# The order of emission in a convolution, attention and mixing kernel: a 3x3 input transform issued step by step, and a prologue whose parts are interleaved

## The chip, the cores and the metric

The kernel runs on one core of one Trainium2 chip. The time is device microseconds of one execution; of several executions the median is given. A core has a matrix engine (TensorE, PE), a vector engine (VectorE, DVE), a scalar engine (ScalarE, ACT), a general engine (GpSimd, POOL) and a sync engine (SyncE, SP) that here only issues DMA transfers. PE writes into PSUM, of which this kernel uses eight banks of 128 x 512 float32; everything else lies in SBUF or in the chip's main memory.

## The reference

Two layers work on eight images of 512 channels and 32 x 32 pixels, all in float32.

```python
# layer 0
x = x + C2f(group_norm(x))
# C2f: t = silu(bn(conv1x1(x))); y0, y1 = two halves of t, 256 channels each
for i in range(2):
    z = silu(bn(conv3x3(y[-1], m_cv1_w[i])))
    q, k, v = conv1x1(z, m_qkv_w[i])             # 4 heads of 64 channels, 1024 positions
    a = softmax(q . (k + rw + rh) * 64 ** -0.5)
    z = silu(bn(conv1x1(a . v, m_cv2_w[i])))
    y.append(y[-1] + z)
out = silu(bn(conv1x1(concat(y), cv2_w)))
# layer 1
x = x + L1(group_norm(x))
# L1: a 1x1 convolution whose weights are scaled by the largest softmax value of each row of S and T,
#     masked where the argmax of S and of T differ, and whose outputs are permuted by p[p], p = argsort(t)
```

Group norm has 32 groups of 16 channels.

## The kernel before, in words

Every image passes the two attention blocks i = 0 and 1. A pair (image, block) is a slot. Images go in pairs, so the order of slots is (0,0), (1,0), (0,1), (1,1), (2,0) and so on, 16 in all. The main loop (from L918) does the attention of slot s in four units: two head pairs times two halves of the query positions. A unit takes eight key tiles. For each, `logits` (L446) makes two logits matmuls into PSUM banks, ACT copies them to SBUF (L459), and DVE takes the running maximum `mx` (L464), which is the last reader of the bank. `top` and `spread` turn the maxima by PE (L472, L480). `soften` (L482) adds the negative maximum on DVE (L484), exponentiates on ACT (L485) and sums on POOL (L490). `values` multiplies by v (L496), and `finish` and `divide` apply the reciprocal of the sum (L508 to L517). DVE's maxima and additions are tied to each other in their order by hand (`in_turn`, L430).

Between the steps of the attention of slot s the loop takes work from `slot_filler` (L824): everything that slot s + 1 needs before its own attention. In order: 8 us of background work; if the next block is 1, the output projection `conv_m2(0)` (L351) and 9 us more of background work; the 3x3 convolution `conv3` (L223); `conv_m2(1)` or 7 us of background work; the projection to q, k and v (`project`, L312); and background work for the rest of a share of 103 us. Background work (`bg.take`) is the first convolution of later images (`First`), the last convolution of layer 0 (`Second`) and layer 1 (`Last`). All of these are Python generators that yield an estimate of the PE time that they have just issued, and a clock of those estimates (`Clock`, L661) starts entries at a given delay (`clock.at`). So the text of the program decides in which order operations are emitted. A framework then plans each engine's own order and all waits; it doesn't keep to the order of emission.

The 3x3 convolution works on groups of four rows in a transformed space (a minimal filtering scheme along the rows). Six input planes u0 to u5 are formed from `ybuf`, the zero-padded image in SBUF, by eight DVE operations for u1 to u4 (L266 to L277) and two on POOL and two on DVE for u0 and u5 (L284 to L287). Each plane goes through 12 matmuls with its transformed weights (`product`, L239) into one bank. Sums and differences of the products (`ss`, `dd`, L288 to L300) give the four output rows y[0] to y[3], and a silu ends it. There are four plane buffers and three buffers for the temporaries a, b, a2, b2. For block 0 `ybuf` is loaded from memory (`load_y`, L217); for block 1 `conv_m2(0)` writes it (L365).

The prologue (L860 to L915) treats images 0 and 1 in turn: load, group norm statistics, normalization, first convolution (`start_conv`). Image 0's conv3 follows, then `positions` (position terms to memory), `last_weights` (L567: layer 1's weights; one-hot masks, ranks and permutations, with four groups of PE work at L605, L609, L624 and L639 to L646), the transformed 3x3 weights of block 1 (`transform_weights`, L544), the first convolution of a half of image 2, and the first `project` and logits. Pools that matter here: ten `st` tiles for logits, which the weights also use; four weight tiles `w`; three half tiles for silu results; five PSUM banks for everything but v's product and the spread maxima.

Of the kernel before, what the change touches and what calls it, by code (L numbers as in the profile page):

```python
# [39 lines left out]
def conv_preact_kernel(ctx: ExitStack, tc: tile.TileContext, x, cv1, cv2, mcv1, qkv, mcv2, bn, rw, rh, conv, s_in, t_in, out):  # L40
# [130 lines left out]
    def accumulate(ps, terms):  # L171
# [6 lines left out]
        return Whole(1.72)  # L178

    class Image:  # L180
        def __init__(self, n):
# [39 lines left out]


        def conv3(self, i):  # L223
            n = self.n
            name = f"{n}_{i}"
            groups = ybuf.rearrange("p c r x -> p (c r x)").rearrange("p (g r x) -> p g r x", r=4, x=F)
            d = [groups[:, 0:NGR, r] for r in range(4)] + [groups[:, 1 : NGR + 1, r] for r in range(2)]

            def temp(nm):
                return wt.tile([P, NGR, F], F32, tag="wt", name=f"{nm}_{name}")  # L230

# [31 lines left out]
            mm, ss, dd = (pair(wm, q, f"{q}_{name}") for q in ("mm", "ss", "dd"))  # L263

            a, b = temp("a"), temp("b")
            stt(a, d[2], -4.0, d[4], ALU.mult, ALU.add)  # L266
            stt(b, d[1], -4.0, d[3], ALU.mult, ALU.add)
            u1, u2 = plane(), plane()
            nc.vector.tensor_tensor(inner(u1), a, b, ALU.add)
            nc.vector.tensor_tensor(inner(u2), a, b, ALU.subtract)  # L270

            a, b = temp("a2"), temp("b2")
            nc.vector.tensor_tensor(a, d[4], d[2], ALU.subtract)
            nc.vector.tensor_tensor(b, d[3], d[1], ALU.subtract)
            u3, u4 = plane(), plane()
            stt(inner(u3), b, 2.0, a, ALU.mult, ALU.add)
            stt(inner(u4), b, -2.0, a, ALU.mult, ALU.add)  # L277
            yield from product(1, u1)
            nc.scalar.copy(mm[:, 0], self.ps)
            yield 1.33  # L280
            yield from product(2, u2)

            u0, u5 = plane(), plane()
            nc.gpsimd.tensor_tensor(inner(u0), d[0], d[2], ALU.subtract)  # L284
            nc.gpsimd.tensor_tensor(inner(u5), d[5], d[3], ALU.subtract)
            stt(inner(u0), inner(u0), 4.0, a, ALU.mult, ALU.add)
            stt(inner(u5), b, -4.0, inner(u5), ALU.mult, ALU.add)  # L287
            nc.vector.tensor_tensor(ss[:, 0], mm[:, 0], self.ps, ALU.add)  # L288
            nc.vector.tensor_tensor(dd[:, 0], mm[:, 0], self.ps, ALU.subtract)
            yield 1.33  # L290
            yield from product(3, u3)
            nc.scalar.copy(mm[:, 1], self.ps)
            yield 1.33
            yield from product(4, u4)
            nc.vector.tensor_tensor(ss[:, 1], mm[:, 1], self.ps, ALU.add)
            nc.vector.tensor_tensor(dd[:, 1], mm[:, 1], self.ps, ALU.subtract)
            stt(y[1], tx(dd[:, 1]), 2.0, tx(dd[:, 0]), ALU.mult, ALU.add)
            stt(y[2], tx(ss[:, 1]), 4.0, tx(ss[:, 0]), ALU.mult, ALU.add)
            nc.vector.tensor_tensor(ss[:, 0], ss[:, 0], ss[:, 1], ALU.add)
            stt(dd[:, 0], dd[:, 1], 8.0, dd[:, 0], ALU.mult, ALU.add)  # L300
            yield 1.33
            yield from product(0, u0)
            nc.vector.tensor_tensor(y[0], tx(self.ps), tx(ss[:, 0]), ALU.add)
            yield 1.33
            yield from product(5, u5)
            nc.vector.tensor_tensor(y[3], tx(self.ps), tx(dd[:, 0]), ALU.add)
            for co in range(IT):
# [259 lines left out]
    def last_weights():  # L567
# [31 lines left out]
        nc.vector.tensor_tensor(lower, gi, wide(idx), ALU.is_gt)  # L599

        oht = pair(stp, "st", "oht")[:NG]
        for a in range(2):
            ps = bank(f"oht_{a}")
            for k in range(CT):
                nc.tensor.transpose(ps[:NG, ts(k, P)], oh[:, CT * a + k], ident)  # L605
            nc.vector.tensor_copy(oht[:, a], ps[:NG])
        for k in range(CT):
            ps = bank(f"mask_{k}")
            nc.tensor.matmul(ps, oht[:, 1, ts(k, P)], oht[:, 0], start=True, stop=True)  # L609
            wk = weff[k // 2][:, k % 2]  # L610
            stt(wk, wk, gain[:, CT + k : CT + k + 1], ps, ALU.mult, ALU.mult)


        tri = small.tile([P, P], F32, tag="tri", bufs=1, name="tri")
# [18 lines left out]
        for k in range(CT):  # L633
            nc.vector.tensor_scalar(perm[k // 2][:, k % 2], io[:, 0], rank[:, k : k + 1], None, ALU.is_equal)
        w1 = [pair(stp, "st", f"w1_{j}") for j in range(2)]
        for o in range(CT):
            ps = bank(f"w1_{o}")
            for k in range(CT):
                nc.tensor.matmul(  # L639
                    ps, perm[k // 2][:, k % 2, ts(o, P)], weff[k // 2][:, k % 2], start=(k == 0), stop=(k == CT - 1)  # L640
                )
            nc.vector.tensor_copy(w1[o // 2][:, o % 2], ps)
        for i in range(CT):
            ps = bank(f"w2_{i}")
# [167 lines left out]
    def call(f, *a):  # L812
        f(*a)
        return
        yield
# [8 lines left out]
    def slot_filler(s):  # L824
# [49 lines left out]
    def start_norm(im, tiles):  # L874
        im.gn0.mean()
        im.gn0.var()
        for h in range(2):
            im.norm_x([tiles[h, kp] for kp in range(2)])

    def start_conv(im, tiles):  # L880
        n = im.n
        for cp in (1, 0):
            w = weights(f"w_cv1_{n}_{cp}", (CT, 256), cv1[cp])
            for h in range(2):
                for co in range(IT):
                    ps = bank(f"cv1_{n}_{cp}_{co}_{h}")
                    us = yield from accumulate(ps, [(w[:, k, ts(co, P)], tiles[h, k // 2][:, k % 2]) for k in range(CT)])
                    t = half_tile(f"y0_{n}_{cp}_{co}_{h}")
# [144 lines left out]
```

## Time and profile before

| quantity | value |
|---|---|
| median of 3 runs (lowest to highest) | 3366.42 us (3352.67 to 3372.92) |
| profiled execution: own time, span | 3359.56 us, 3357.8 us |
| PE, share of the span busy | 95% |
| DVE, ACT, POOL | 62%, 53%, 37% |
| granted PE clock, mean | 0.98 of full |
| first logits matmul | 219.39 us after the start |
| input transform, one operation of 128 x 544 | 0.72 us, up to 1.80 us |

Times in the profile are microseconds from the start of the span unless a column says nanoseconds. A line of the timeline has start, duration, engine, source line, operation, what it writes and reads, and in brackets how long the engine was idle ahead of it and which instruction ended that. A line of waits has the waiting engine and line, the releaser, the total, the number and the longest. PE's float32 matmuls count as two records each. A line of the table by stretch has the stretch, its length, the busy time of each engine with its instructions, the granted PE clock, the share of the DMA engines and GB/s.

### The profile page before, as it was taken

What the parts mean: (1) busy time and instruction counts of PE and PEld (TensorE: products, weight loads), DVE (VectorE), ACT (ScalarE), POOL (GpSimd) and SP (SyncE); (2) the same over time, 40 slices, a digit from 0 to 9 for tenths busy, and PEclk for the clock granted to TensorE, in tenths of its full rate; (3) what the DMA queues carried; (4) which work ended last, traced back from release to release, by engine and by line L of the source; (5) the groups of instructions that cost most, each with busy time, mean ns of one, the idle gap of its engine ahead of it and who ended that gap; (6) DMA issues with size and microseconds to landing.
All of it is one profiled execution on the core that took longest, in us unless ns stands there. A gap on an engine that the chain in (4) does not pass through costs nothing.

```text
span 3357.8 us, 33292 instructions
## 1 busy us (share of the span) xinstructions
PE 3185.7 (95%) x11716; PEld 1549.4 (46%) x11716; DVE 2074.0 (62%) x2717; ACT 1764.3 (53%) x2371; POOL 1237.1 (37%) x971
## 2 busy tenths in 40 slices
PE   6999989999999999999999999999999999999998
PEld 2645435353545445354545445354545445353343
DVE  4335666576766576676766675776656675766642
ACT  3035685755564654644555555644455554645631
POOL 2004333344443344334444343344334333444420
PEclk9899999999999999999999999999999999999999
DMA  7553343230222341432222341423232341423366
GB/s 273 211 176 128 109 152 110 96 118 34 101 92 93 104 138 46 146 109 101 101 101 94 122 144 54 138 100 110 91 109 93 116 144 54 155 72 107 110 212 204
DMA packets 142294, 400.34 MB, mean 119 GB/s; under 512 B 13104, under 2 KB 14384, under 8 KB 142128
## 3 DMA queue, kind: packets, MB, share of 16 engines
q1 hardware_dynamic: 141408, 397.99, 34.7%
q8 instruction: 93, 1.52, 0.2%
q14 instruction: 73, 0.60, 0.1%
q10 hardware_dynamic: 720, 0.23, 0.0%
HBM read 318.47 MB, written 79.69 MB: 119 GB/s over the span
## 4 chain that ended last, share of the span: by engine, by line
PE 68%; DVE 11%; issue 6%; ACT 4%; DMA 3%; POOL 1%; SPq 0%; POOLq 0%; DVEq 0%; ACTq 0%
PE cv L175 13%; PE po L496 11%; PE m L245 11%; PE lg L453 11%; PE qk L175 6%; PE l L175 6%; PE v L340 3%; DVE st L484 2%; PE mt L472 2%; PE den L508 2%; DVE mx L464 2%; PE mb L480 2%; PE m L175 2%; DVE rb L515 1%; DMA res<-y 1%
## 5 line engine op out<-in xcount | busy, mean ns | idle before, releaser
L490 POOL TENSOR_TENSOR sum<-sum,st 128x512 f32<-128x512 f32 x768 | 993.9, 1324 | 759.8 <-ACT st L485 759.8
L485 ACT ACTIVATE st<-st 128x1024 f32<-128x1024 f32 x512 | 536.2, 1056 | 526.3 <-DVE st L484 519.0
L464 DVE TENSOR_TENSOR mx<-mx,lg 128x512 f32<-128x512 f32 x768 | 479.5, 681 | 413.5 <-ACT st L459 413.2
L484 DVE TENSOR_TENSOR st<-st,mb 128x1024 f32<-128x1024 f32 x512 | 604.9, 1214 | 88.2 <-PE mb L480 88.2
L459 ACT COPY st<-lg 128x512 f32<-128x512 f32 x1024 | 527.2, 595 | 204.3 <-PE lg L453 163.9
L245 PE MATMUL m<-plane,w_m 128*128 128x256 f32 x2304 | 541.3, 390 | 31.0 <-DVE mx L464 16.9
L453 PE MATMUL lg<-q,k 64*128 64x512 f32 x2048 | 535.7, 619 | 10.5 <-ACT y L130 3.3
L496 PE MATMUL po<-st,v 128*64 128x512 f32 x2048 | 512.5, 612 | 9.3 <-ACT st L485 5.4
L245 PEld LDWEIGHTS m<-plane,w_m 128*128 128x128 f32 x2304 | 436.7, 194 | 153.0 <-issue 47.6
L490 POOL TENSOR_TENSOR sum<-st,st 128x512 f32<-128x512 f32 x128 | 160.3, 1274 | 876.6 <-ACT st L485 616.8
L175 PE MATMUL cv<-y,w_cv 128*128 128x512 f32 x1024 | 467.5, 601 | 3.5 <-DMA y<-y 2.0
L453 PEld LDWEIGHTS lg<-q,k 64*128 64x128 f32 x2048 | 189.9, 186 | 348.9 <-issue 216.5
L175 PEld LDWEIGHTS cv<-y,w_cv 128*128 128x128 f32 x1024 | 185.3, 190 | 251.4 <-issue 234.2
L496 PEld LDWEIGHTS po<-st,v 128*64 128x64 f32 x2048 | 125.6, 137 | 330.3 <-issue 252.1
L175 PE MATMUL cv<-x,w_cv 128*128 128x512 f32 x512 | 241.6, 620 | 30.6 <-ACT x L165 15.8
L515 DVE RECIPROCAL rb<-rb 128x256 f32<-128x256 f32 x128 | 216.0, 1725 | 70.8 <-ACT rb L510 70.8
L175 PE MATMUL l<-x,w_l 128*128 128x512 f32 x512 | 239.5, 614 | 18.7 <-DVE mx L464 13.6
L175 PE MATMUL qk<-z,w_qkv 128*128 128x512 f32 x512 | 235.0, 601 | 9.2 <-DVE mx L464 9.2
L473 DVE TENSOR_REDUCE nm<-mt 128x4 f32<-128x512 f32 x128 | 82.9, 685 | 193.3 <-PE mt L472 193.0
L175 PEld LDWEIGHTS cv<-x,w_cv 128*128 128x128 f32 x512 | 96.6, 197 | 156.8 <-issue 109.5
L130 ACT ACT_TABLE_LOAD x123 | 157.8, 1283 | 19.4 <-PE cv L175 8.1
L175 PEld LDWEIGHTS l<-x,w_l 128*128 128x128 f32 x512 | 94.8, 194 | 143.2 <-issue 105.0
(144 smaller groups left out, 2387.9 us busy)
## 6 DMA issues: line engine op xcount, KB each, us to landing
w_m<-w_m SPq DMA_DIRECT2D x96, 768.0 KB, 4.3
w_cv<-in_cv SPq DMA_DIRECT2D x92, 512.0 KB, 3.5
y<-y SPq DMA_DIRECT2D x64, 512.0 KB, 4.9
x<-in_x SPq DMA_DIRECT2D x56, 512.0 KB, 5.0
y<-y SPq DMA_DIRECT2D x64, 256.0 KB, 3.5
k<-r SPq DMA_DIRECT2D x32, 512.0 KB, 3.7
res<-y SPq DMA_DIRECT2D x32, 512.0 KB, 4.2
xr<-in_x SPq DMA_DIRECT2D x32, 512.0 KB, 4.1
```

The source lines that it names most:

```text
L130: nc.scalar.activation(dst, src, AF.Silu, bias=bn_b[:, col : col + 1], scale=bn_s[:, col : col + 1])
L175: nc.tensor.matmul(ps, w, moving, start=(n == 0), stop=(n == len(terms) - 1))
L245: nc.tensor.matmul(ps[:, ts(co, 256)].rearrange("p (t x) -> p t x", x=F), w[:, co, c, dx], u[:, 9 * c : 9 * c + 8, dx : dx + F], start=(j ...
L340: nc.tensor.matmul(ps[:, ts(j, P)], z[:, c, ts(4 * j4 + j, P)], w[:, c, 512 + P * hp : 512 + P * hp + P], start=(c == 0), stop=(c == IT - 1),)
L453: nc.tensor.matmul(lg[h], self.k[r, ts(t, P)], self.q[r, self.hp, ts(self.half, HALF)], start=True, stop=True)
L459: nc.scalar.copy(st[:, h], lg[h])
L464: in_turn(nc.vector.tensor_tensor(self.mx[:, h], so_far[:, h], lg[h], ALU.max))
L484: in_turn(nc.vector.tensor_tensor(st, st, flat(self.mb), ALU.add))
L485: nc.scalar.activation(st, st, AF.Exp)
L490: nc.gpsimd.tensor_tensor(self.acc[:, h], so_far[:, h], self.st[t][:, h], ALU.add)
L496: nc.tensor.matmul(self.po[HD * h : HD * h + HD], self.v[:, t, ts(h, HD)], self.st[t][:, h], start=(t == 0), stop=(t == KT - 1),)
L515: nc.vector.reciprocal(self.rb[:, r], self.rb[:, r])
```

## The change

The change leaves every arithmetic operation as it is and emits some of them elsewhere. A class `Spread` holds a list of operations: each is due at a delay plus a multiple of a gap on the clock, and `upto(n)` emits the first n at once if they aren't out yet.

- The eight transform operations for u1 to u4 become `Image.transform`, a `Spread`. For block 1 it starts 3 us after `conv_m2(0)` with gaps of 1.0; for block 0 `load_y` and the transform are emitted at the end of the slot before, with a delay of 8 and gaps of 1.3. `conv3` asks for the first 3 at its start, 4 before product 2 and 8 after it.
- The two sums of product 2 come ahead of u0 and u5.
- The four sums after product 4 become a `Spread`, of which two must be out after product 0 and all after product 5. The order of y[1] and y[2] is exchanged.
- `last_weights` becomes a generator with yields, advanced at every third yield of image 0's conv3.
- The prologue loads image 1 ahead of image 0's first convolution and emits its group norm, and the weights' transform of block 0, at clock times within it. Both images share one load of the first convolution's weights. Image 2's loads and statistics (`bg.prepare`) come ahead of conv3. Image 1's `load_y` and transform come after image 0's `project`.

```diff
+    class Spread:
+        def __init__(self, ops, delay, gap):
+            self.ops, self.done = ops, 0
+            for n in range(len(ops)):
+                clock.at(delay + gap * n, lambda n=n: self.upto(n + 1))
+
+        def upto(self, n):
+            while self.done < n:
+                self.done += 1
+                self.ops[self.done - 1]()
...
+        def transform(self, i, delay, gap):
...
+            self.inputs = Spread(
+                [
+                    lambda: stt(temp("a"), d[2], -4.0, d[4], ALU.mult, ALU.add),
+                    lambda: stt(temp("b"), d[1], -4.0, d[3], ALU.mult, ALU.add),
+                    lambda: tt(plane(1), t["a"], t["b"], ALU.add),
+                    lambda: tt(plane(2), t["a"], t["b"], ALU.subtract),
+                    lambda: tt(temp("a2"), d[4], d[2], ALU.subtract),
+                    lambda: tt(temp("b2"), d[3], d[1], ALU.subtract),
+                    lambda: stt(plane(3), t["b2"], 2.0, t["a2"], ALU.mult, ALU.add),
+                    lambda: stt(plane(4), t["b2"], -2.0, t["a2"], ALU.mult, ALU.add),
+                ],
+                delay,
+                gap,
+            )
...
         def conv3(self, i):
...
+            self.inputs.upto(3)
+            t, d = self.t, self.d
...
-            a, b = temp("a"), temp("b")
...
-            stt(inner(u4), b, -2.0, a, ALU.mult, ALU.add)
-            yield from product(1, u1)
+            yield from product(1, t[1])
             nc.scalar.copy(mm[:, 0], self.ps)
             yield 1.33
-            yield from product(2, u2)
-
+            self.inputs.upto(4)
+            yield from product(2, t[2])
+            self.inputs.upto(8)
+            a, b = t["a2"], t["b2"]
+
+            nc.vector.tensor_tensor(ss[:, 0], mm[:, 0], self.ps, ALU.add)
+            nc.vector.tensor_tensor(dd[:, 0], mm[:, 0], self.ps, ALU.subtract)
             u0, u5 = plane(), plane()
             nc.gpsimd.tensor_tensor(inner(u0), d[0], d[2], ALU.subtract)
             nc.gpsimd.tensor_tensor(inner(u5), d[5], d[3], ALU.subtract)
             stt(inner(u0), inner(u0), 4.0, a, ALU.mult, ALU.add)
             stt(inner(u5), b, -4.0, inner(u5), ALU.mult, ALU.add)
-            nc.vector.tensor_tensor(ss[:, 0], mm[:, 0], self.ps, ALU.add)
-            nc.vector.tensor_tensor(dd[:, 0], mm[:, 0], self.ps, ALU.subtract)
...
-            stt(y[1], tx(dd[:, 1]), 2.0, tx(dd[:, 0]), ALU.mult, ALU.add)
-            stt(y[2], tx(ss[:, 1]), 4.0, tx(ss[:, 0]), ALU.mult, ALU.add)
-            nc.vector.tensor_tensor(ss[:, 0], ss[:, 0], ss[:, 1], ALU.add)
-            stt(dd[:, 0], dd[:, 1], 8.0, dd[:, 0], ALU.mult, ALU.add)
+            sums = Spread(
+                [
+                    lambda: stt(y[2], tx(ss[:, 1]), 4.0, tx(ss[:, 0]), ALU.mult, ALU.add),
+                    lambda: nc.vector.tensor_tensor(ss[:, 0], ss[:, 0], ss[:, 1], ALU.add),
+                    lambda: stt(y[1], tx(dd[:, 1]), 2.0, tx(dd[:, 0]), ALU.mult, ALU.add),
+                    lambda: stt(dd[:, 0], dd[:, 1], 8.0, dd[:, 0], ALU.mult, ALU.add),
+                ],
+                1.0,
+                1.3,
+            )
             yield 1.33
             yield from product(0, u0)
+            sums.upto(2)
...
             yield from product(5, u5)
+            sums.upto(4)
...
         nc.vector.tensor_tensor(lower, gi, wide(idx), ALU.is_gt)
 
+        yield
         oht = pair(stp, "st", "oht")[:NG]
...
             nc.vector.tensor_copy(oht[:, a], ps[:NG])
+        yield
         for k in range(CT):
             ps = bank(f"mask_{k}")
...
+        yield
...
+        yield
         w1 = [pair(stp, "st", f"w1_{j}") for j in range(2)]
...
             nc.vector.tensor_copy(w1[o // 2][:, o % 2], ps)
+            if o % 2:
+                yield
...
-        if im and i == 0:
-            add(0.0, call(im.load_y))
         add(8.0, bg.take(8.0))
         if im and i == 1:
             add(7.0, im.conv_m2(0))
+            add(0.0, call(im.transform, 1, 3.0, 1.0))
             add(9.0, bg.take(9.0))
...
             add(21.0, im.project(i))
+        if s + 2 < len(slots) and slots[s + 2][1] == 0:
+            add(0.0, call(slots[s + 2][0].load_y))
+            add(0.0, call(slots[s + 2][0].transform, 0, 8.0, 1.3))
...
     tiles = start(first, gx, "gx")
+    w = [weights(f"w_cv1_{cp}", (CT, 256), cv1[cp]) for cp in (1, 0)][::-1]
+    first.gn0.mean()
+    first.gn0.var()
     start_norm(first, tiles)
-    clock.run(start_conv(first, tiles))
+    tiles2 = start(second, gy, "gy")
+    clock.at(5.0, second.gn0.mean)
+    clock.at(9.0, second.gn0.var)
+    clock.at(11.0, lambda: start_norm(second, tiles2))
+    clock.at(12.0, lambda: transform_weights(0))
+    clock.run(start_conv(first, tiles, w))
     first.load_y()
-    tiles = start(second, gy, "gy")
-    transform_weights(0)
-    start_norm(second, tiles)
-    clock.run(start_conv(second, tiles))
     bg.add(*(First(m, h) for m in images[2:] for h in range(2)))
     held = [bg.items.pop()]
-    clock.run(first.conv3(0))
+    clock.run(start_conv(second, tiles2, w))
     positions(0)
-    last_weights()
+    bg.prepare()
+    first.transform(0, 0.0, 0.0)
+    side = last_weights()
+    for n, us in enumerate(first.conv3(0)):
+        clock.tick(us)
+        if n % 3 == 0:
+            next(side, None)
+    for _ in side:
+        pass
     transform_weights(1)
     positions(1)
     clock.run(bg.take(7.0, force=True))
     clock.run(first.project(0))
+    second.load_y()
+    second.transform(0, 8.0, 1.3)
```

More of the change, by code (lines that the diff above doesn't have):

```diff
@@ L220, in load_y, with temp, plane @@
                 load(ybuf[:, c, 1 : F + 1].rearrange("p r x -> p (r x)"), y_dram[self.n][1][:, c])
+        def transform(self, i, delay, gap):
+            name = f"{self.n}_{i}"
+            groups = ybuf.rearrange("p c r x -> p (c r x)").rearrange("p (g r x) -> p g r x", r=4, x=F)
+            d = self.d = [groups[:, 0:NGR, r] for r in range(4)] + [groups[:, 1 : NGR + 1, r] for r in range(2)]
+            tt = nc.vector.tensor_tensor
+            t = self.t = {}
+            def temp(nm):
+                t[nm] = wt.tile([P, NGR, F], F32, tag="wt", name=f"{nm}_{name}")
+                return t[nm]
+            def plane(r):
+                plane_count[0] += 1
+                t[r] = planes[plane_count[0] % 4]
+                return t[r][:, :, 1 : F + 1]
+            self.inputs = Spread(
[12 more added lines that the diff above has]
+            )
         def conv3(self, i):
@@ L225, in conv3 @@
             name = f"{n}_{i}"
[L226 to L230, printed above, removed]
+            self.inputs.upto(3)
+            t, d = self.t, self.d
             def plane():
@@ L263, in conv3 @@
             mm, ss, dd = (pair(wm, q, f"{q}_{name}") for q in ("mm", "ss", "dd"))
-            a, b = temp("a"), temp("b")
[L266 to L276, printed above, removed]
-            stt(inner(u4), b, -2.0, a, ALU.mult, ALU.add)
-            yield from product(1, u1)
+            yield from product(1, t[1])
             nc.scalar.copy(mm[:, 0], self.ps)
             yield 1.33
-            yield from product(2, u2)
+            self.inputs.upto(4)
[4 more added lines that the diff above has]
+            nc.vector.tensor_tensor(dd[:, 0], mm[:, 0], self.ps, ALU.subtract)
             u0, u5 = plane(), plane()
@@ L287, in conv3 @@
             stt(inner(u5), b, -4.0, inner(u5), ALU.mult, ALU.add)
-            nc.vector.tensor_tensor(ss[:, 0], mm[:, 0], self.ps, ALU.add)
-            nc.vector.tensor_tensor(dd[:, 0], mm[:, 0], self.ps, ALU.subtract)
             yield 1.33
-            yield from product(3, u3)
+            yield from product(3, t[3])
             nc.scalar.copy(mm[:, 1], self.ps)
             yield 1.33
-            yield from product(4, u4)
+            yield from product(4, t[4])
             nc.vector.tensor_tensor(ss[:, 1], mm[:, 1], self.ps, ALU.add)
             nc.vector.tensor_tensor(dd[:, 1], mm[:, 1], self.ps, ALU.subtract)
-            stt(y[1], tx(dd[:, 1]), 2.0, tx(dd[:, 0]), ALU.mult, ALU.add)
-            stt(y[2], tx(ss[:, 1]), 4.0, tx(ss[:, 0]), ALU.mult, ALU.add)
-            nc.vector.tensor_tensor(ss[:, 0], ss[:, 0], ss[:, 1], ALU.add)
-            stt(dd[:, 0], dd[:, 1], 8.0, dd[:, 0], ALU.mult, ALU.add)
+            sums = Spread(
[8 more added lines that the diff above has]
+            )
             yield 1.33
             yield from product(0, u0)
+            sums.upto(2)
             nc.vector.tensor_tensor(y[0], tx(self.ps), tx(ss[:, 0]), ALU.add)
@@ L874, in start_norm, with start_conv @@
     def start_norm(im, tiles):
-        im.gn0.mean()
-        im.gn0.var()
         for h in range(2):
             im.norm_x([tiles[h, kp] for kp in range(2)])
-    def start_conv(im, tiles):
+    def start_conv(im, tiles, w):
         n = im.n
         for cp in (1, 0):
-            w = weights(f"w_cv1_{n}_{cp}", (CT, 256), cv1[cp])
             for h in range(2):
@@ L886, in start_conv @@
                     ps = bank(f"cv1_{n}_{cp}_{co}_{h}")
-                    us = yield from accumulate(ps, [(w[:, k, ts(co, P)], tiles[h, k // 2][:, k % 2]) for k in range(CT)])
+                    terms = [(w[cp][:, k, ts(co, P)], tiles[h, k // 2][:, k % 2]) for k in range(CT)]
+                    us = yield from accumulate(ps, terms)
                     t = half_tile(f"y0_{n}_{cp}_{co}_{h}")
```

## The prediction, made before the result was known

> **What bounds the kernel now.** I read the page first. TensorE is the only engine near its limit:
>
> ```profile
> span 3357.8 us, 33292 instructions
> ...
> PE 3185.7 (95%) x11716; PEld 1549.4 (46%) x11716; DVE 2074.0 (62%) x2717; ACT 1764.3 (53%) x2371; POOL 1237.1 (37%) x971
> ```
>
> So an engine other than PE matters only where it makes PE wait: 3357.8 - 3185.7 = 172 us in all. The waits of PE by releaser (total us, times, longest) say who ends them:
>
> ```profile
> PE gm_a L146 <- DVE mv_a L144: 20.5, 3, 14.4
> PE m L175 <- ACT m2s L130: 17.1, 6, 3.7
> PE m L245 <- DVE mx L464: 16.9, 7, 4.2
> PE cv L175 <- ACT x L165: 15.8, 3, 11.1
> PE l L175 <- DVE mx L464: 13.6, 5, 4.7
> PE m L245 <- ACT st L485: 13.5, 3, 4.6
> ...
> PE mask L609 <- DVE oht L606: 6.0, 1, 6.0
> ```
>
> The timeline of PE (start, us, operation, idle ahead of it) places them. Before the first softmax:
>
> ```profile
> 62.47 29.98 PE L175 MATMUL cv<-x,w_cv 128*128 128x512 f32 x64 [11.06 <-ACT x L165]
> ...
> 130.40 7.19 PE L609 MATMUL mask<-oht 16*128 16x512 f32 x8 [5.98 <-DVE oht L606]
> ...
> 150.85 16.43 PE L639 MATMUL w<-weff,perm 128*128 128x512 f32 x32 [2.06 <-DVE perm L634]
> ...
> 185.29 12.84 PE L175 MATMUL cv<-x,w_cv 128*128 128x512 f32 x24 [2.39 <-ACT x L165]
> ```
>
> An idle stretch costs more than itself. In the table of busy time by stretch the granted clock (before the DMA share) is half after a gap and full some 5 us later:
>
> ```profile
> 62.40:67.00 4.60, 4.54 (x6) 1.95 (x7) 1.61 (x5) 4.60 (x8) 0.00 (x0) 0.50 1.09 330
> 130.00:138.00 8.00, 7.60 (x11) 2.97 (x11) 4.65 (x8) 1.56 (x2) 0.00 (x0) 0.50 0.58 216
> 150.80:156.00 5.20, 5.15 (x7) 2.23 (x8) 1.18 (x3) 0.84 (x1) 0.00 (x0) 0.52 0.43 151
> 156.00:160.00 4.00, 4.00 (x11) 1.85 (x10) 0.69 (x1) 0.00 (x0) 0.00 (x0) 1.00 0.00 0
> ```
>
> In the steady part the input transform runs in one piece on DVE, with the row maxima (mx, which free the logits' banks) behind it. DVE, then PE:
>
> ```profile
> 1418.03 1.68 DVE L266 SCALAR_TENSOR_TENSOR a<-ybuf 128x544 f32<-128x544 f32 x1
> 1419.63 1.79 DVE L267 SCALAR_TENSOR_TENSOR b<-ybuf 128x544 f32<-128x544 f32 x1
> ...
> 1426.15 0.68 DVE L464 TENSOR_TENSOR mx<-mx,lg 128x512 f32<-128x512 f32 x1
> ...
> 1426.89 3.78 PE L175 MATMUL l<-x,w_l 128*128 128x512 f32 x4 [3.47 <-DVE mx L464]
> ```
>
> **What the Trainium skill says.** "TensorE: Matmul & The Clock Gate", Part 1: The HAM clock gate, gives a cold array half the clock until it has been busy for about 3.4 us. The trace agrees: 0.50 for 4 to 5 us after the gaps above. "SBUF — State Buffer", SBUF: two separate sides: a DVE operation with two SBUF inputs and a GpSimd operation that reads SBUF exclude each other for a whole instruction. The trace agrees: the transform's operations take 0.72 us, but 1.68 to 1.79 while POOL adds exponentials (L490, 1417.59 to 1424.26). "Perfetto Trace Analysis", Per-instruction lifecycle, calls ACT, DVE and GpSimd strict FIFO. The trace agrees: at 54.42 POOL's 1.0 us power for the group norm starts only behind a weight addition (L556) that waited for a DMA.
>
> **What order the trace shows.** The order on an engine isn't that of the text. L587, from the last layer's weights, runs at 9.94 us; image 2's transform for the convolution at 832 us begins at 720. An operation goes early wherever it is ready and its engine had a gap in the plan; the place of emission only ranks what is ready together. This decides which parts of the change can move anything.
>
> **The change, part by part.**
>
> (A) Group norm of the second image inside the first convolution. Its sums were ready at 23.1 us (last L144), but the averaging matmul stands behind the whole convolution, at 48.26. Then come 2.51 and 11.06 us of idle PE, and 4.6 us at half clock (2.3 lost): 15.9 us removed. Added: nothing new. The 8 applications (5.75 us of ACT) lie between silus, with ACT busy 17 of the first 50 us; uncovered they would cost those 5.75. Moved ahead of the last y stores on SP: transform_weights(0) issues 6 loads and 12 stores there, and 6 ACT copies (0.83), 10 DVE (0.95) and 2 POOL operations (1.8). It ran there already (its loads at 11.1 and 42.8), so I take 0. If SP stops on a store, silu results back up: 3 half tiles and 5 banks, eight results of 3.4 us, 27 us before PE feels it; bound 0 to 8 us. Two loads of 512 KB vanish. Conv3 then starts at about 76 instead of 92.3; its first weights left at 62.92 (4.3 us to land), so 9 us of slack remain.
>
> (B) The last layer's weights in pieces among conv3's products. Idle removed: 5.98 + 2.06. Half clock removed: 7.1 us of mask and 4.8 us of L639, so 3.5 + 2.4. The rank products between them (51 matmuls, 11.3 us at half clock): between 0 and half of that, 5.6; I take 2.8, because their weight loads of 0.55 us a pair look clock-bound but no warm ones are shown. Sum 16.7. PE's work is unchanged. Each piece's result is wanted three yields (4 us) later, covering the 2.5 us of L606's copies. Against it: narrow rank products may cool the clock for the next products, 0 to 2.3.
>
> (C) Image 2's loads, mean and variance ahead of conv3: 1.39 + 2.39 us idle and 5 us at 0.51 (2.4): 6.2 us. The four loads already ran at 79 to 114.
>
> A + B + C = 38.8 us. I count 32, since a removed wait usually shows a smaller one (a bank behind a silu, conv3's weights).
>
> (D) The transform one operation at a time, block 1 (8 times). Idle PE during its pieces: 3.64, 1.72, 4.46, 3.47, 4.62, 4.69, 4.46, 3.46 = 30.5 us; seven are long enough for a cold clock, 1.7 to 2.5 us each (0.66 over 5 us, 0.50 over 5 us), about 14. Open to gain: 44.5. But the run of 8 starts 0.03 us after the last ybuf addition (1418.03 after 1417.32 + 0.68), as early as the data allow. Emission 3 to 10 us after conv_m2 instead of after 9 us of filling work doesn't separate operations that the planner already pulls forward. It ranks them higher, which helps the three places where PE waited for the first plane (4.5 us each, labelled ACT st L485) and hurts the maxima. From 0 to 44.5 I take a quarter, 11; a loss is the third rival.
>
> (E) The four sums after product 4. They run as one piece ahead of the next softmax addition (1283.29 to 1287.94, then L484). With the pause after the first, the addition outranks the other three. Idle there: 1.52, 1.40, 2.65, 2.04, 2.04, 2.04 = 11.7, plus 3 x 1.7 of clock: 17. I take half, 8.5, because where the additions aren't ready the order stays.
>
> (F) Load of y and transform for block 0 in the slot before. Both SP loads (512 KB, 7.1 us to land) pass that slot's last background loads; they already go as soon as ybuf is free, 100 us ahead. Stalls there: 4.21 and 2.54, about 8 with the clock. Gain 0 to 8, taken 0. A transform at DVE's head that waits for the load holds the maxima and additions behind it. (G) The two sums of product 2 ahead of u0 and u5: DVE waited 29 us for POOL there, but PE shows next to none of it: 0.
>
> Sum: 32 + 11 + 8.5 = 51.5 us. The profiled execution took 3359.56 us (1.76 around its span); less 51.5 it is 3308.1. The median of the three runs (3352.67 to 3372.92) is 6.9 above the profiled one, so I predict 3315.
>
> **The rivals.** First, only the prologue gains: the planner places DVE's work as before and D to F give nothing, 20 to 38.8 us: about 3334 from the median. For it speaks the order described above; against it that the sums (E) have an explicit competitor. Second, everything goes: 38.8 + 44.5 + 17 + 8 = 108 us, 3258. For it speaks that DVE is 62% busy, so the work fits; against it that operations of 1.8 us still block the queue. Third, slower: the transform, now ranked above the maxima, goes ahead of them in all 15 steady conv3s, and block 0's waits at DVE's head for y. Today's D and F stalls cost 53. At 4.6 + 1.7 us each, 15 would cost 94, a net gain of the change hardly touched by the prologue's 32 (-32 + 41 = +9). It decides from (53 + 32) / 15 = 5.7 us per conv3; at 9 us (the 7.1 us landing plus a cold clock of 1.9) it is +50, so 3416. Against it: in the six steady cases DVE waited only 14.2 us for that load (34.5 in all, less 13.5 and 6.8 in the prologue). That the change doesn't do what it says is half of the first rival: spread in the text, unspread on the engine.
>
> **The numbers.** Forecast (38 to 70 us gained) 0.45; prologue alone 0.30; all of it 0.13; slower 0.12. One per cent is 34 us, about what a measurement of this kernel tells from no change. Faster by more: the forecast, the second rival and little of the first, 0.60; slower by more: most of the third, 0.10; between them 0.30. The range goes from 3275, inside the second rival, to 3362, past the first with its bounds on SP; it leaves out the third and the far end of the second, 2 in 10.
>
> **What would show it.** Right: the second convolution starts at about 48.5 with full clock; the first mask matmul has no idle before it; the first logits come near 187 instead of 219.4; between sums a softmax addition (L484) stands on DVE; planes and maxima still in long runs for block 1. Wrong: logits still after 205 (SP or banks held the prologue); no run of more than three transform operations and no PE wait above 2 us near conv3 (second rival); more and longer PE waits on mx and DVE waiting on ybuf (third). The weakest assumption is the planner's order, which I infer from one trace.

## The result, and the profile after

The kernel after takes 3331.99 us (median of 6 runs, 3329.67 to 3343.57), the kernel before, run beside it, 3361.93 us (median of 6, 3352.67 to 3372.92). The ratio is 0.9914 with a 95% interval of 0.9891 to 0.9937: about 30 us, 0.9%, faster. The profiled execution has a span of 3328.0 us.

The page of the kernel after, its span and the busy times:

```profile
span 3328.0 us, 33287 instructions
...
PE 3177.4 (95%) x11716; PEld 1541.6 (46%) x11716; DVE 2069.0 (62%) x2717; ACT 1763.7 (53%) x2371; POOL 1238.7 (37%) x971
```

PE's time without work is now 150.6 us (3328.0 - 3177.4), 21.5 less than before; its busy time fell by another 8.3 us, though it issues the same 11716 matmuls. That part is stretches at half clock that are gone.

The waits of PE from 220 us to 3330 us, after the prologue (waiting line, releaser, total us, times, longest):

```profile
PE m L289 <- DVE mx L505: 18.6, 7, 4.2
PE m L175 <- ACT m2s L130: 17.1, 6, 3.7
PE mt L513 <- DVE mx L505: 13.8, 3, 4.6
PE l L175 <- DVE mx L505: 12.3, 5, 3.5
```

Read it beside the list of before (L289 was L245, L505 was L464, L526 was L485). Three of the four are rows of before within 2 us. One row went, the convolution's product on ACT st (13.5 us, 3 times). One came: mt, the transposes of the finished maxima, on mx (13.8 us, 3 times). So the steady part swapped one wait for another of the same size.

The prologue did change. Timeline of PE in the kernel after (start, us, operation, idle ahead of it):

```profile
59.62 16.90 PE L175 MATMUL cv<-x,w_cv 128*128 128x512 f32 x39
78.30 5.42 PE L289 MATMUL m<-plane,w_m 128*128 128x256 f32 x24 [1.77 <-DMA w_m<-w_m]
...
86.22 4.12 PE L289 MATMUL m<-plane,w_m 128*128 128x256 f32 x18 [1.63 <-DMA w_m<-w_m]
...
90.40 3.69 PE L652 MATMUL mask<-oht 16*128 16x512 f32 x8
94.02 5.84 PE L289 MATMUL m<-plane,w_m 128*128 128x256 f32 x18
...
106.07 7.06 PE L289 MATMUL m<-plane,w_m 128*128 128x256 f32 x18
...
186.40 1.99 PE L494 MATMUL lg<-q,k 64*128 64x512 f32 x8
```

The second image's convolution joins the first without a gap. The first mask matmul has no idle ahead of it and takes 3.69 us instead of 7.19. Two new waits stand on conv3's weights. The first logits start at 186.40 instead of 219.39 us: 33.0 us earlier. From there to the end the kernel takes 3328.0 - 186.40 = 3141.6 us; before it took 3357.8 - 219.39 = 3138.4. **The prologue gives everything, and the remaining 94% of the kernel nothing.**

The table by stretch (stretch, length, busy PE, PEld, DVE, ACT, POOL, granted clock, DMA share, GB/s) of the kernel after:

```profile
44.00:50.00 6.00, 6.00 (x15) 2.66 (x14) 5.71 (x3) 0.78 (x1) 4.70 (x3) 1.00 0.49 182
106.00:112.00 6.00, 6.00 (x16) 4.83 (x16) 4.71 (x13) 0.43 (x1) 0.00 (x0) 0.50 0.25 87
```

At the seam of the two convolutions the clock is full, where it was 0.50 after the gap of 11.06 us. But a new stretch at half clock stands at 106 us, just behind the rank products. The 7.06 us of the row at 106.07 are conv3's products in it; the same 18 records take 4.12 us at 86.22. That is 3 us. A shorter one, from 95 to 98 us, stands behind the mask products: the 18 records at 94.02 take 5.84 us, 1.7 more.

**Why the transform gave nothing.** DVE in the kernel after, where conv_m2 of a block 1 has just written ybuf; it answers the lines at 1418 us shown of before. Then PE:

```profile
1386.70 0.69 DVE L406 TENSOR_TENSOR ybuf<-res,m2s 128x512 f32<-128x512 f32 x1
1387.42 1.68 DVE L256 SCALAR_TENSOR_TENSOR a<-ybuf 128x544 f32<-128x544 f32 x1
1389.02 1.79 DVE L257 SCALAR_TENSOR_TENSOR b<-ybuf 128x544 f32<-128x544 f32 x1
1390.74 1.79 DVE L261 TENSOR_TENSOR a<-ybuf 128x544 f32<-128x544 f32 x1
1392.45 1.78 DVE L258 TENSOR_TENSOR plane<-a,b 128x544 f32<-128x544 f32 x1
...
1395.55 0.68 DVE L505 TENSOR_TENSOR mx<-mx,lg 128x512 f32<-128x512 f32 x1
...
1396.28 3.78 PE L175 MATMUL l<-x,w_l 128*128 128x512 f32 x4 [3.53 <-DVE mx L505]
```

The text issues these at least 1.0 us of estimated PE work apart. On the engine six of them (L259 and L262 are the two left out) still run end to end from the moment ybuf is written, even L261 ahead of L258, and the maximum waits behind them. PE's wait is 3.53 us; before it was 3.47. Issuing an operation later in the text didn't make it run later. In four of block 1's eight transforms, this one among them, DVE's order is that of before to the last operation, and in a fifth one operation moved; the three others made the swap of waits above.

### The profile page after: what moved, and what is told of

It reads as the page before. It is cut to its first block, busy times and chain, and to the rows that moved or that the text cites. A ratio compares the mean times of both kernels' runs of the same rounds, so it can differ in the third digit from the quotient of the medians.

```text
span 3328.0 us, 33287 instructions
## 1 busy us (share of the span) xinstructions
PE 3177.4 (95%) x11716; PEld 1541.6 (46%) x11716; DVE 2069.0 (62%) x2717; ACT 1763.7 (53%) x2371; POOL 1238.7 (37%) x971
## 4 chain that ended last, share of the span: by engine, by line
PE 69%; DVE 10%; issue 6%; ACT 5%; DMA 3%; POOL 1%; SPq 0%; POOLq 0%; DVEq 0%; ACTq 0%
PE cv L175 14%; PE po L537 11%; PE m L289 11%; PE lg L494 11%; PE qk L175 6%; PE l L175 6%; PE v L381 3%; DVE st L525 2%; PE mt L513 2%; PE den L549 2%; PE m L175 2%; DVE mx L505 2%; PE mb L521 2%; ACT st L526 1%; DVE rb L556 1%
## 5 line engine op out<-in xcount | busy, mean ns | idle before, releaser
L526 ACT ACTIVATE st<-st 128x1024 f32<-128x1024 f32 x512 | 536.2, 1056 | 516.9 <-DVE st L525 509.6
L505 DVE TENSOR_TENSOR mx<-mx,lg 128x512 f32<-128x512 f32 x768 | 479.2, 680 | 412.6 <-ACT st L500 412.2
L525 DVE TENSOR_TENSOR st<-st,mb 128x1024 f32<-128x1024 f32 x512 | 604.4, 1212 | 88.3 <-PE mb L521 88.3
L289 PE MATMUL m<-plane,w_m 128*128 128x256 f32 x2304 | 540.3, 388 | 24.3 <-DVE mx L505 18.6
L494 PE MATMUL lg<-q,k 64*128 64x512 f32 x2048 | 538.4, 620 | 10.6 <-ACT y L130 3.4
L537 PE MATMUL po<-st,v 128*64 128x512 f32 x2048 | 511.5, 611 | 7.5 <-ACT st L526 5.1
L289 PEld LDWEIGHTS m<-plane,w_m 128*128 128x128 f32 x2304 | 434.7, 193 | 148.9 <-issue 52.7
L494 PEld LDWEIGHTS lg<-q,k 64*128 64x128 f32 x2048 | 189.8, 186 | 349.3 <-issue 218.2
L537 PEld LDWEIGHTS po<-st,v 128*64 128x64 f32 x2048 | 125.7, 137 | 328.3 <-issue 250.0
L175 PE MATMUL l<-x,w_l 128*128 128x512 f32 x512 | 239.5, 614 | 17.0 <-DVE mx L505 12.3
```

The source lines that it names most:

```text
L175: nc.tensor.matmul(ps, w, moving, start=(n == 0), stop=(n == len(terms) - 1))
L289: nc.tensor.matmul(ps[:, ts(co, 256)].rearrange("p (t x) -> p t x", x=F), w[:, co, c, dx], u[:, 9 * c : 9 * c + 8, dx : dx + F], start=(j ...
L494: nc.tensor.matmul(lg[h], self.k[r, ts(t, P)], self.q[r, self.hp, ts(self.half, HALF)], start=True, stop=True)
L505: in_turn(nc.vector.tensor_tensor(self.mx[:, h], so_far[:, h], lg[h], ALU.max))
L525: in_turn(nc.vector.tensor_tensor(st, st, flat(self.mb), ALU.add))
L526: nc.scalar.activation(st, st, AF.Exp)
```

## The experiments

Ratios are to the kernel before, run on the same chip; "us gained" is (1 - ratio) x 3362. Runs on different chips are compared by these ratios.

### The prologue alone, and the rest alone

The first theory: the prologue gives all, because the emission place of the other parts doesn't reach the engine. The rival: D and E do gain, and the prologue gives less. One kernel has only the changed prologue, with conv3 as before; the other has the changed conv3 and slot order, with the old prologue.

```diff
 # prologue only, against after
-        def transform(self, i, delay, gap):
...
-            self.inputs.upto(3)
+            stt(a, d[2], -4.0, d[4], ALU.mult, ALU.add)
...
 # rest only, against after
-    tiles2 = start(second, gy, "gy")
-    clock.at(5.0, second.gn0.mean)
...
+    clock.run(start_conv(first, tiles))
+    first.load_y()
+    tiles = start(second, gy, "gy")
+    transform_weights(0)
+    start_norm(second, tiles)
```

> The kernel before with the changed prologue alone (image 1's group norm inside the first convolution, the last layer's weights among conv3's products, image 2's loads first); input transform and sums as before. Theory 1 (the whole gain is the prologue's, the steady part gained nothing): first logits near 186.5 us as after the whole change (219.4 before), the rest of the span as long as before (3138 us), span 3325 us, 0.990 of before, no slower than the whole change. Rival (the steady edits gain too, or cost): first logits near 186.5 but the rest differs from that of before by what the steady edits don't give, total 5 us or more away from the whole change's 3328.

> The whole change without its prologue: input transform and sums one operation at a time, block 0's load of y and transform in the slot before, prologue as before. Theory 1: first logits near 219, PE idle near the 3x3 convolutions as long as before (about 49 us in stalls over 1.3 us), span 3358 to 3362 us, 1.000 of before within 0.3 per cent. Rival (the steady edits gain something that the changed prologue then takes away): 3340 us or less.

Prologue only: 3333.76 us, ratio 0.9922 (0.9905 to 0.9939), 26 us, first logits at 189.03. The rest only: 3363.45 us, ratio 1.0002 (0.9994 to 1.0009): nothing, within 3 us. Together they give what the whole change gives. PE's waits in the rest-only kernel have the exchange seen above:

```profile
PE m L289 <- DVE mx L505: 17.4, 7, 4.2
PE mt L513 <- DVE mx L505: 13.8, 3, 4.6
```

and in the prologue-only kernel it is the old one:

```profile
PE m L245 <- DVE mx L464: 18.6, 7, 4.2
PE m L245 <- ACT st L485: 13.4, 3, 4.5
```

So D to G carry the exchange, and it is worth zero.

### Tied to the softmax order

If the planner undoes the spacing, a tie should make it work. `in_turn` adds a scheduling dependency on the softmax operation emitted before, as the maxima and additions have it already. The first kernel ties every operation of a `Spread`; the second also widens the gaps.

```diff
         def upto(self, n):
             while self.done < n:
                 self.done += 1
-                self.ops[self.done - 1]()
+                in_turn(self.ops[self.done - 1]())
 # the second kernel, besides
-            add(0.0, call(im.transform, 1, 3.0, 1.0))
+            add(0.0, call(im.transform, 1, 3.0, 2.4))
...
                 1.0,
-                1.3,
+                3.5,
```

> The changed kernel with every operation of the transform and of the sums tied into the hand-made order of the maxima and additions on DVE, at the place where it is emitted. Theory 2 (the planner pulls the operations together, so the spacing of emission never reached the engine): runs of transform operations split at softmax operations, PE waits on maxima near conv3 fall to half, 25 us less than the changed kernel, near 3303. Rival (the emission itself isn't spread: all four sums and four transform operations are due within one step of the softmax loop, so tying them changes nothing or puts the softmax additions behind them): within 6 us of the changed kernel, with the 2.0 us waits after the sums still there or longer.

> As the tied kernel, but with gaps of 2.4 instead of 1.0 for block 1's transform and 3.5 instead of 1.3 for the sums, so that at most three of these operations stand between two softmax groups. Theory 3 (PE waits because a run of 6 to 9 us on DVE holds the maxima; three operations are short enough): the waits of 3.5 and 4.6 us ahead of or in block 1's conv3 and the 2.0 us waits after the sums go, 25 to 40 us less than the changed kernel, 3288 to 3303. Rival (the waits are shifted to the next operation of DVE or to the planes that conv3 then waits for): within 10 us of the changed kernel, with waits of PE on plane additions instead.

Tied: 3299.88 us, 0.9819 (0.9801 to 0.9837), 61 us gained. Tied with wide gaps: 3285.06 us (3282.88 to 3289.39), 0.9774 (0.9755 to 0.9793), 76 us gained: **faster than both kernels**. The arithmetic and the places of emission in the first are those of the change; only the ties differ. They are worth 32 us, and with the gaps 47 us, beyond the 29 of the change itself.

The same place as above, block 1 behind the last ybuf addition, which here ends at 1376.50, DVE in the kernel tied with wide gaps:

```profile
1376.53 0.72 DVE L256 SCALAR_TENSOR_TENSOR a<-ybuf 128x544 f32<-128x544 f32 x1
1377.17 2.35 DVE L525 TENSOR_TENSOR st<-st,mb 128x1024 f32<-128x1024 f32 x2
1379.44 0.72 DVE L257 SCALAR_TENSOR_TENSOR b<-ybuf 128x544 f32<-128x544 f32 x1
1384.84 2.48 DVE L505 TENSOR_TENSOR mx<-mx,lg 128x512 f32<-128x512 f32 x4 [4.69 <-ACT st L500]
1387.24 0.72 DVE L258 TENSOR_TENSOR plane<-a,b 128x544 f32<-128x544 f32 x1
```

Additions and maxima stand between the pieces, and DVE even has 4.69 us with nothing to do. Here the first pieces take 0.72 us and not 1.7 to 1.8. Over the whole kernel the 128 transform operations take 121.8 us instead of 135.4, and 24 of them more than 1.4 us instead of 40. The Trainium skill, "SBUF — State Buffer", SBUF: two separate sides, says that such a DVE operation and a GpSimd one that reads SBUF exclude each other. The traces agree: each of the 40 slow ones and each of these 24 overlaps POOL instructions for more than 60% of its time. So the spread pieces meet POOL less often; what that alone is worth wasn't tried apart. PE's waits from 220 to 3330 us in this kernel:

```profile
PE m L175 <- ACT m2s L130: 14.8, 6, 2.5
PE po L537 <- ACT st L526: 11.4, 6, 4.4
PE l L175 <- DVE mx L505: 8.2, 7, 1.6
```

m on mx (18.6 us) and mt on mx (13.8 us) have left the list, and l on mx is down from 12.3 to 8.2. From the first logits to the end it takes 3287.6 - 188.05 = 3099.6 us, 42 less than after. PE's waits there fell from 124.5 to 93.9 us in all, 31 of the 42; the other 11 are less busy time for the same matmuls, at a mean granted clock over the span of 0.989 instead of 0.985.

### Is it the tie or the gap, and which operations?

Three kernels separate the two: wide gaps with no tie; only the transforms tied (gap 2.4); only the sums tied (gap 3.5).

```diff
-            add(0.0, call(im.transform, 1, 3.0, 1.0))
+            add(0.0, call(im.transform, 1, 3.0, 2.4))
...
 # the other two: a flag of Spread
-                self.ops[self.done - 1]()
+                instruction = self.ops[self.done - 1]()
+                if self.bound:
+                    in_turn(instruction)
```

> The changed kernel with the wider gaps (2.4 and 3.5) but nothing tied. Theory (gaps reach the engine only when the operations are tied): DVE's order near conv3 stays that of the changed kernel but for a few places, the same 3.5, 4.6 and 2.0 us waits, within 8 us of the changed kernel (0.989 to 0.993 of before). Rival (the gaps alone suffice, since a later emission ranks a sum below the next softmax addition): most of the tied kernel's gain, 0.980 of before or less.

> The changed kernel with the transform alone tied and at gaps of 2.4; the sums as in the changed kernel. If the gain of the tied wide kernel (43 us by the medians) divides as the idle near conv3 did (30.5 us by block 1's transforms and 6.8 by block 0's, 11.7 by the sums, each with its cold clock): 33 us less than the changed kernel, near 3299. Rival (most of it is the sums): 3320 or more.

> The changed kernel with the sums alone tied and at gaps of 3.5; the transform as in the changed kernel. By the same division: 11 us less than the changed kernel, near 3321, with the three 2.0 us waits after the sums gone and the 3.5 and 4.6 us waits at block 1's transform still there. Rival: 3305 or less, the transform's waits gone too.

| kernel | median us | ratio (95%) | us gained |
|---|---|---|---|
| the change as it is | 3331.99 | 0.9914 (0.9891 to 0.9937) | 29 |
| wide gaps, no tie | 3326.82 | 0.9895 (0.9871 to 0.9920) | 35 |
| only transforms tied, wide | 3293.44 | 0.9788 (0.9770 to 0.9805) | 71 |
| only sums tied, wide | 3319.50 | 0.9863 (0.9848 to 0.9878) | 46 |
| both tied, wide | 3285.06 | 0.9774 (0.9755 to 0.9793) | 76 |

In total the gap alone is not distinguishable from the change: the intervals overlap, and PE still waits 13.9 us in mt on mx, as it did. DVE in the kernel with wide gaps and no tie keeps the run in the same order as after, though each two are 2.4 us of emission apart (the first two of six):

```profile
1386.58 1.68 DVE L256 SCALAR_TENSOR_TENSOR a<-ybuf 128x544 f32<-128x544 f32 x1
1388.18 1.79 DVE L257 SCALAR_TENSOR_TENSOR b<-ybuf 128x544 f32<-128x544 f32 x1
```

For the four sums it is otherwise. With 3.5 us between them and no tie, a softmax addition (L525) stands between the sums in 11 of the 16 conv3s, where the change has it in one, and the three PE waits of 2.04 us behind them, which the expectation had kept, are gone. DVE, then PE, in the same kernel:

```profile
1253.99 0.68 DVE L332 SCALAR_TENSOR_TENSOR z<-ss 128x512 f32<-128x512 f32 x1
1254.59 1.21 DVE L525 TENSOR_TENSOR st<-st,mb 128x1024 f32<-128x1024 f32 x1
1255.72 0.68 DVE L333 TENSOR_TENSOR ss<-ss 128x512 f32<-128x512 f32 x1
...
1260.41 4.15 PE L289 MATMUL m<-plane,w_m 128*128 128x256 f32 x18 [0.36 <-DVE mx L505]
```

So the transform needs the tie; a gap of 3.5 us reaches the sums without one. Most of the gain is in the transforms: tied and with the wide gap they give 42 us beyond the change, and the sums 17. Beyond the wide gaps without a tie it is 36 and 11 us, and for the sums the two intervals still touch. Both together give 47 us beyond the change and not 59; the 12 us between lie within the intervals.

### Block 1 alone, and gaps that are too wide

```diff
 # block 1 alone: tied, gap 2.4
+                bound=i == 1,
 # too wide: everything tied
-            add(0.0, call(im.transform, 1, 3.0, 1.0))
+            add(0.0, call(im.transform, 1, 3.0, 3.6))
...
-            add(0.0, call(slots[s + 2][0].transform, 0, 8.0, 1.3))
+            add(0.0, call(slots[s + 2][0].transform, 0, 8.0, 2.6))
...
                 1.0,
-                1.3,
+                5.0,
```

> As the kernel with the transform alone tied at gaps of 2.4, but tied for block 1 only; block 0's transform is left to the planner. The prediction's list put 44.5 us of idle and cold clock on block 1 and 8 on block 0. If that is the division, at least 31 of the 38 us that tying both gave stay, near 3300. Rival (block 0's operations, pulled into the conv3 of the slot before, cost more than their own stalls show): 3310 or more.

> The tied wide kernel with still wider gaps: 3.6 for block 1's transform (2.4), 2.6 for block 0's (1.3), 5.0 for the sums (3.5). If the length of the run on DVE were all, one or two operations between softmax groups would bring a few us more, 3278 to 3284. Rival (PE then waits for planes and sums, which come late): 3287 or more, with PE's waits ahead of conv3's matmuls (m) longer than the 1.85 us of the tied wide kernel.

Block 1 alone: 3302.93 us, 0.9825 (0.9807 to 0.9842), 59 us gained. That is 30 beyond the change; tying block 0's transforms too brings 12 more.

Too wide: 3312.40 us (3311.46 to 3315.32), 0.9856 (0.9836 to 0.9877), 48 us gained, so 28 less than with the smaller gaps. PE's waits, then its timeline, name a part of it:

```profile
PE m L289 <- DVE plane L258: 11.4, 4, 3.6
```

```profile
1217.98 2.86 PE L289 MATMUL m<-plane,w_m 128*128 128x256 f32 x12 [2.62 <-DVE plane L258]
```

As its rival had it, PE now waits for planes: the first plane is late for its product. These 11.4 us are new, but other waits shrank: all of PE's idle time rose by only some 6 us (114.2 to 120.5). Its busy time rose by 15 (3167.9 to 3183.2), at a mean clock of 0.988 instead of 0.989. By line, 8.6 of the 15 us lie in the products with v (L537), 5.0 in conv3's (L289) and 4.1 in the logits (L494), with small falls elsewhere; why they take longer isn't settled.

### The three parts of the prologue, each by itself

A (image 1's norm within the first convolution), B (the last layer's weights among conv3's products) and C (image 2's loads and statistics ahead of conv3), each alone on the kernel before, in a single run. The kernel before took 3357.63 us beside them, 6 us under its median of 3363.49 in 23 runs, so the first logits are compared and not the times.

```diff
 # A alone
+    clock.at(5.0, second.gn0.mean)
+    clock.at(9.0, second.gn0.var)
+    clock.at(11.0, lambda: start_norm(second, tiles2))
+    clock.at(12.0, lambda: transform_weights(0))
 # B alone
-    last_weights()
+    side = last_weights()
+    for n, us in enumerate(first.conv3(0)):
+        clock.tick(us)
+        if n % 3 == 0:
+            next(side, None)
 # C alone
+    bg.prepare()
```

> The kernel before with part A alone: image 1's loads, group norm and the weights' transform inside image 0's first convolution, first-convolution weights loaded once. By the prediction's sum A removes 11.06 + 2.51 us of idle and 2.3 us of half clock: second convolution at 48.5 instead of 62.5, first logits at 219.4 - 15.9 = 203.5 us. Rival (the last y stores wait behind the weights' stores, or conv3 now waits for its own weights): first logits 2 to 8 us later than that, and an idle stretch ahead of conv3.

> The kernel before with part B alone: the last layer's weights in pieces among conv3's products. By the prediction's sum 8.0 us of idle and 8.7 us of half clock go, of them 2.8 us in the rank products: first logits at 219.4 - 16.7 = 202.7 us. Rival (the clock falls again during the narrow rank products, or conv3's pieces wait): 206 us or later with a granted clock of 0.5 behind the rank products.

> The kernel before with part C alone: image 2's loads, mean and variance emitted ahead of conv3. By the prediction's sum 3.8 us of idle and 2.4 us of half clock go: first logits at 219.4 - 6.2 = 213.2 us. Rival (the loads then pass conv3's own weights on the queue and conv3 waits for them): 219 us or later with a wait of PE on w_m.

| kernel | first logits at, us | earlier by | predicted | span, us |
|---|---|---|---|---|
| A alone | 193.71 | 25.7 | 15.9 | 3335.5 |
| B alone | 207.37 | 12.0 | 16.7 | 3348.6 |
| C alone | 214.65 | 4.7 | 6.2 | 3353.0 |
| all three, conv3 as before | 189.03 | 30.4 | 38.8, counted 32 | 3329.7 |
| all three, in the change | 186.40 | 33.0 | | 3328.0 |

A is larger than its part of the sum, because it takes a piece of B's. The mask's wait falls from 5.98 to 1.09 us with A alone, and the mask from 7.19 to 5.58. What the 5.98 us were stands in DVE's timeline of the kernel before:

```profile
125.92 0.72 DVE L266 SCALAR_TENSOR_TENSOR a<-ybuf 128x544 f32<-128x544 f32 x1 [6.84 <-DMA ybuf<-y]
...
129.07 1.27 DVE L606 COPY oht<-oht 16x512 f32<-16x512 f32 x2
```

The copies of the one-hot masks stood behind image 1's transform, and that stood at DVE's head for the load of y. With A alone the order is the other way round: the copies run right behind their transposes, at 106.90, and that transform at 127.09, without a wait. The wait on perm ahead of L639 falls too, from 2.06 to 1.04 us. B and C are smaller, because a later wait grows or comes: with B alone PE waits 7.23 us for image 2's statistics, where it was 1.39; with C alone those waits are gone and one of 2.51 us stands at image 3's statistics. The parts sum to 42.4 us and give 30.4 together with conv3 as before, 33.0 in the change. In the eight kernels with the changed prologue and the new conv3 the first logits lie between 183.09 and 188.05 us, so a difference below 5 us, C's too, says little.

## Why the prediction was right or wrong

Forecast 3315, measured 3332; predicted gain 51.5 us, measured 30. The time lies within the stated range because that range (3275 to 3362) was wide enough to hold the first rival; the forecast's own band, 38 to 70 us gained, was missed. Of the 51.5 us the 32 of the prologue came, and the 19.5 of D and E did not. There is luck in the distance too: counted from the median of the six runs and not of the first three, the forecast is 3310, 22 us off. The steps in their order:

**A, B and C, counted 32 after a discount of 6.8 from their sum.** Right in total, 33.0 (30.4 with conv3 as before), as the logits show (predicted near 187, measured 186.40). The discount was the right step and its reason held: a removed wait showed a smaller one. The terms of A and B were mis-sized: 15.9 and 16.7 against 25.7 and 12.0 alone (C: 6.2 against 4.7). They aren't independent: of B's 16.7 us, most of the 5.98 was DVE held by a transform at its head, and A alone ends that.

- That the second convolution starts at about 48.5 with full clock: right in what mattered. It joins the first, and the clock is 1.00 from 44 to 50 us.
- "9 us of slack" for conv3's first weights: wrong. PE waits 1.77 and 1.63 us for the weights at 78.30 and 86.22. From 78 to 90 us the DMA engines are busy for 0.98 of the time, at 372 GB/s. With A alone conv3 starts at 75.00 without a wait, which points to the image loads that C brings ahead of it; C's transfers were costed only by what they take away.
- 0 for the y stores behind the loads of A (bound 0 to 8 us): the stop is there, ACT has 4.66 us idle at 56.64 us on a store of y, and PE shows no wait from it.
- Rank products that cool the clock for the next products, 0 to 2.3 us: they do, and cost 3 us; the mask products do too, 1.7 us. Together that is twice the bound. Against it, the rank products themselves fell from 11.3 to 6.4 us, 4.9 where 2.8 had been taken.

**D, a quarter of 44.5 us: the failed step.** The quarter was taken although the prediction had said that emission "doesn't separate operations that the planner already pulls forward". It said too that the three first-plane waits would be helped and the maxima hurt. Both happened, at a ratio of one to one: three waits of 4.5 us are gone, and three of 4.6 us came. The first of them, DVE and PE in the kernel before; the product starts when the first plane is written:

```profile
1240.86 0.72 DVE L269 TENSOR_TENSOR plane<-a,b 128x544 f32<-128x544 f32 x1
...
1241.67 4.28 PE L245 MATMUL m<-plane,w_m 128*128 128x256 f32 x12 [4.46 <-ACT st L485]
```

PE now idles 0.56 us before conv3's first product, but 4.59 us before the transposes behind it. DVE, then PE, in the kernel after:

```profile
1212.74 1.19 DVE L262 TENSOR_TENSOR b<-ybuf 128x544 f32<-128x544 f32 x1
1213.96 1.67 DVE L263 SCALAR_TENSOR_TENSOR plane<-b,a 128x544 f32<-128x544 f32 x1
1215.55 2.47 DVE L505 TENSOR_TENSOR mx<-mx,lg 128x512 f32<-128x512 f32 x4
...
1208.18 2.83 PE L289 MATMUL m<-plane,w_m 128*128 128x256 f32 x12 [0.56 <-issue]
...
1217.47 1.71 PE L513 MATMUL mt<-ident,mx 128*128 128x128 f32 x8 [4.59 <-DVE mx L505]
```

The operation for u3 (L263), which ran behind the maxima before, now runs directly ahead of them. The value to take was 0, as the rest-only kernel shows (ratio 1.0002). The stall itself was real: block 1 tied with the wide gap gives 30 us beyond the change, of the 44.5 that were called open.

**E, half of 17 us: failed too, but for another reason.** The order of the four sums changed (y[2] first), but in 15 of the 16 conv3s they still run as one piece ahead of the addition. DVE in the kernel after (the third and fourth, L333 and L335, are left out):

```profile
1254.30 0.68 DVE L332 SCALAR_TENSOR_TENSOR z<-ss 128x512 f32<-128x512 f32 x1
1254.90 1.76 DVE L334 SCALAR_TENSOR_TENSOR z<-dd 128x512 f32<-128x512 f32 x1
...
1258.86 1.21 DVE L525 TENSOR_TENSOR st<-st,mb 128x1024 f32<-128x1024 f32 x1
```

The prediction had named an L484 addition between sums as its sign; it stands there in one conv3 of 16, and PE's wait behind the sums above is 2.04 us, as before. The "explicit competitor" didn't take the slot, because a pause of 1.3 us is too short for it: with 3.5 us and no tie it does in 11 of 16. Tied with that gap the sums give 17 us beyond the change, about what was called open. (One wait in that sum, 1.40 us at 730 us, stands ahead of the sums and not behind them.)

**F, 0, and G, 0:** right. The rest-only kernel holds D to G together, and they give nothing within 3 us. That block 0's transform has its 8 us open was right in kind: tied it brings about 12.

**The rivals.** What came is the first one (only the prologue gains, 3334): the measured 3332 is 2 us off it. It had a chance of 0.30, and its own argument was the stronger one: the order that the trace shows. Nothing of the second (everything goes) came by itself, but the tied kernel with wide gaps, 3285 us, goes two thirds of the way to it. The third (slower) found its mechanism in three places and not in 15, and in each another wait went.

Not settled: which rule of the planner pulls a ready operation forward. The runs show only that for the transform a tie overrides it and gaps of 1.0 and 2.4 us in the emission do not, and that for the sums 1.3 us is too little and 3.5 enough.

## What to carry to other kernels

Where a framework plans each engine's order, look in the trace whether a pause in the emission shows on the engine. Here one of 3.5 us showed and one of 1.3 us did not; where operations already started the instant that their input was written, no pause that was tried spaced them, and an ordering dependency on the neighbours did. Moving the pieces of a run without spacing them only chose which of the waiters behind it paid. Waits of a serial prologue are not summed: measure each part alone. Here parts of 42 us gave 30 to 33.

## What was not expected of the hardware

- Small products cool the array though it never idles. In the kernel after the granted clock is 0.50 from 106 to 112 us, directly behind the rank products (16 columns wide), with PE busy for all of the 6.00 us; 18 records take 7.06 us instead of 4.12. It is 0.50 from 95 to 98 us too, behind the mask products (16 of 128 rows), again with PE busy throughout. Such products didn't warm it either: in the kernel before, the clock fell at 128 us, in the wait ahead of the masks, and stayed at 0.50 until 155 us, through 18.4 us of mask and rank products. So the half clock at 150.8 us, which the prediction reads behind a wait of 2.06 us, had begun earlier. The Trainium skill, "TensorE: Matmul & The Clock Gate", Part 1: The HAM clock gate, speaks of a busy array as a warm one; here busy in the profile was not enough.
- A wait shorter than the 3.4 us of idle after which the same section has the array cold can also lower the clock: before, it is 1.00 from 1280 us to the wait of 2.04 us ahead of the product at 1291.40, and 0.50 from 1292.42 to 1295.83. It needn't: the two other waits of 2.04 us at the same place of a conv3 (2040.8 and 2791.6) have none behind them.
